# A state-space layer, routed experts, attention and a Kronecker MLP on one core: the last expert slot joins the tokens by one-hot products, and softplus is summed in PSUM by VectorE

## The chip, the core and the metric

The kernel runs on one NeuronCore of a Trainium2 chip. Its engines work side by side, each from its own in-order queue: TensorE (PE in the profile, with its weight loads as PEld), VectorE (DVE), ScalarE (ACT), GpSimd (POOL) and SyncE (SP, which issues most DMAs; ACT and POOL issue some too). The metric is device time in microseconds. Everything is float32. A measurement of this kernel can tell about 0.3% from no change.

## The reference, cut to what matters

Input x is (4, 384, 32, 32): four batches of 384 channels and 1024 positions. Two layers follow, each a token mixer and a channel mixer, with normalisation ahead and a residual around each.

```python
# layer 0, mixer: four directions k of a selective scan over 1024 positions, 16 states
dt = softplus(dts + dt_projs_bias)             # (4, 4, 384, 1024)
h  = h * exp(dt * A) + (dt * u) * B            # per position, (b, k, 384, 16)
y  = einsum('bkdn,bkn->bkd', h, C)
x  = x + gelu(layernorm(merge(y + D * u)))
# layer 0, experts: four experts 384 -> 1536 -> 384, two for each token
probs  = softmax(t @ gate_w + gate_b);  masked = top-2 of probs, normalised
t = t + sum_e masked[e] * (gelu(t_n @ w1[e] + b1[e]) @ w2[e] + b2[e])
# layer 1: attention of 8 heads with one projection for q, k and v, then an MLP
t = t + mlp(ln(x + attention(ln(x))))
```

## The kernel before

**Two strands.** `scan_layer` runs the scan of batch 0, then of 1, 2 and 3. `tail_batch` does the rest for one batch: routing (`route`, `spread`, `places`), experts (`experts`), the sum of each token's two expert rows (`combine`), attention, and the last layers. The tail of batch b-1 stands in the program behind the scan of batch b and runs beside scans; the tail of batch 3 runs at the end, in a second set of buffers (`wide`). The order of instructions on each engine isn't the order of the code: the program is built with `schedule_with_timeline_sim=True`, and a planner orders it by a simulated timeline, by the order of the code where several are ready, and `high_priority(offset=FORWARD)` moves a block ahead. Tiles that share a tag share a number of buffers (`NARROW`, `WIDE`), which are handed out as they come free; `got`, the weights `w1` and `w2`, and others share "kw" (8 buffers, 10 in `wide`), and `xs`, `xc`, `y`, `diag`, `ex` and others share "k4" (5, and 4 in `wide`).

**A scan.** It is cut into units of one direction and one half of the positions, eight for a batch, and each unit into three pieces of 128 channels (`chunk`), 24 pieces a batch. While one unit runs, `project` prepares the next. For a piece: a product gives the step sizes before softplus in a PSUM bank (`dt_ps`, L365); softplus is computed as max(z, 0) + ln(1 + e) + (e - ((1 + e) - 1)) with e = exp(-|z|), where the last bracket restores what rounding 1 + e lost; the result and its product with u go to HBM and come back spread over states (`dtr`). ScalarE makes |z| (L369), max(z, 0) (L370), e (L371), 1 + e (L372), its logarithm (L373). In batch 0 the terms are added in PSUM by identity products (L378). In the other batches ScalarE forms (1 + e) - 1 (L382), GpSimd makes two subtractions (L395, L396), and VectorE one addition in PSUM (L402). `behind` places the GpSimd and VectorE parts behind an instruction of the running piece. Then `chunk` does, for four groups of states: products on GpSimd (L440, L468), exponentials on ScalarE (L449), scans and products on VectorE (L454, L461), and sums over states on TensorE (L475).

**Routing.** `clear` writes zeros to a list of 2432 rows in HBM (`rows`, 19 writes of 128 rows). `places` finds for each token and each of its two experts a row, so that each block of 256 or 128 rows belongs to one expert. `spread` normalises the tokens and scatters each to its two rows (L685, 16 indirect DMAs on GpSimd).

**Experts.** There are 11 slots: 8 of 256 rows and 3 of 128. For each, `fetch` loads the weights of its expert and `gather` loads its rows and transposes them; then the first product (L954), Gelu, the second (L975), an addition of the bias (L979), and the rows are written to HBM (`made`, L982). The last slot's write is issued by ScalarE, the others by SyncE.

**Combine.** Two diagonal matrices of the gates are made on GpSimd (L996), 16 indirect DMAs on GpSimd fetch each token's two rows from `made` (L1005); they depend on all writes to `made`. `add` puts them onto the residual: two products with the diagonals (L1012) and an addition (L1015) for each 128 tokens, followed by the statistics for the next normalisation (L1037, L1038) in `prologue`.

**Attention.** Its row sums of exponentials are kept for all batches in `sums`; `overflow` takes one maximum of them at the end.

## Time and profile before

| what | value |
|---|---|
| median of 3 runs | 4249.24 us (4240.75 to 4253.25) |
| profiled execution | 4230.72 us |
| its span | 4228.9 us |
| scans 0, 1, 2, 3 (first to last product on GpSimd) | 30 to 685, 683 to 1557, 1557 to 2508, 2508 to 3408 us |
| experts of batches 0 to 3 (first to last product) | 862 to 1298, 1825 to 2257, 2793 to 3218, 3503 to 3930 us |
| first projection of attention, batches 0 to 3 | 1353, 2313, 3284, 3965 us |

A busy time is that of instructions in flight on an engine; matmul ends are modelled, and a product of float32 is recorded as two passes. In a group of instructions, "out<-in" names what is written and read, followed by the count, the busy time, the mean of one, and the idle time of the engine just before with what ended it. In an answer by windows each row has the stretch, its length, then busy time (and count) of PE, PEld, DVE, ACT and POOL, the granted clock, the DMA share and GB/s.

### The profile page before, as it was taken

The page shows a single profiled execution, that of the slowest core. Times are in us where ns is not written, and L with a number is a line of the kernel's source. Part 1 is how long each engine was busy: PE and PEld are TensorE (multiplying, and loading weights), DVE is VectorE, ACT ScalarE, POOL GpSimd, SP SyncE. Part 2 cuts the span into 40 slices and gives each one's busy share as a digit, 9 for nine tenths or more (in the row PEclk, how much of TensorE's full clock was granted, in tenths as well). Part 3 has the DMA queues.
Part 4 walks back from the last instruction along what each step waited for, and adds up shares of the span by engine and source line. Part 5 has one row for each costly group of instructions (what it writes and reads, how often), then busy time and mean ns, then how long its engine had stood idle before and what let it go on. Part 6 is the DMA issues. An engine that isn't in the chain of part 4 may idle for free.

```text
span 4228.9 us, 45721 instructions
## 1 busy us (share of the span) xinstructions
PE 3363.3 (80%) x13308; PEld 1581.4 (37%) x13308; DVE 2846.4 (67%) x4152; ACT 2505.9 (59%) x4494; POOL 3020.1 (71%) x1471
## 2 busy tenths in 40 slices
PE   6544545489897888789996888789996899999898
PEld 2111111155553223245553223245553235566323
DVE  5999997878887878788887777888886840010101
ACT  5555555556665776666665777676664763443353
POOL 5999997898988978789899878889897840000100
PEclk8666666589998999789997999789997899999999
DMA  5454464677886535667887434658887434255200
GB/s 138 125 135 123 117 174 109 187 218 218 242 249 176 153 106 147 198 178 230 251 247 220 130 100 133 200 166 242 227 250 225 117 107 143 86 174 209 64 16 31
DMA packets 410387, 693.70 MB, mean 164 GB/s; under 512 B 51088, under 2 KB 209680, under 8 KB 410128
## 3 DMA queue, kind: packets, MB, share of 16 engines
q1 hardware_dynamic: 399728, 662.71, 54.1%
q0 software_dynamic: 8192, 25.17, 1.8%
q10 hardware_dynamic: 2208, 2.82, 0.2%
q8 instruction: 107, 1.75, 0.2%
q14 instruction: 152, 1.25, 0.1%
HBM read 569.00 MB, written 121.50 MB: 163 GB/s over the span
## 4 chain that ended last, share of the span: by engine, by line
PE 37%; DVE 22%; ACT 11%; DMA 11%; POOL 9%; issue 7%; SPq 3%; DVEq 0%; POOLq 0%; ACTq 0%
PE y_ps L975 9%; PE h_ps L954 9%; DVE da L454 8%; DVE bx L454 7%; POOL bx L440 5%; DMA dtr<-dd 4%; ACT da L449 3%; PE s_ps L1099 3%; PE acc L475 3%; DVE bx L461 3%; PE o_acc L1145 3%; POOL bx L468 2%; DMA w<-in_w 2%; SPq L424 2%; DMA bcs<-both 1%
## 5 line engine op out<-in xcount | busy, mean ns | idle before, releaser
L440 POOL TENSOR_TENSOR bx<-dtr,bcs 128x1024 f32<-128x1024 f32 x768 | 1794.0, 2363 | 201.6 <-PE acc L475 92.4
L449 ACT ACTIVATE da<-dtr,nega 128x512 f32<-128x512 f32 x1536 | 1045.3, 690 | 898.3 <-DVE bx L461 540.9
L468 POOL TENSOR_TENSOR bx<-bx,bcs 128x1024 f32<-128x1024 f32 x384 | 905.1, 2362 | 133.3 <-DVE carry L465 60.5
L475 PE MATMUL acc<-bx,sel 128*32 128x512 f32 x3072 | 500.2, 697 | 294.0 <-POOL bx L468 256.8
L954 PE MATMUL h_ps<-xc,w 128*128 128x256 f32 (+1 forms) x3168 | 675.8, 370 | 71.0 <-DMA w<-in_w 40.0
L975 PE MATMUL y_ps<-w,hs 128*128 128x384 f32 x1824 | 634.4, 500 | 26.7 <-ACT hs L967 20.1
L954 PEld LDWEIGHTS h_ps<-xc,w 128*128 128x128 f32 x3168 | 561.0, 201 | 240.7 <-issue 120.2
L454 DVE TENSOR_TENSOR_SCAN bx<-da,carry,bx 128x512 f32<-128x512 f32 x384 | 473.5, 1270 | 112.9 <-ACT da L449 57.7
L454 DVE TENSOR_TENSOR_SCAN da<-da,carry,bx 128x512 f32<-128x512 f32 x384 | 477.3, 1275 | 60.9 <-ACT da L449 50.2
L454 DVE TENSOR_TENSOR_SCAN bx<-da,bx 128x512 f32<-128x512 f32 x384 | 453.5, 1211 | 90.4 <-ACT da L449 56.8
L461 DVE TENSOR_TENSOR bx<-da,bcs 128x512 f32<-128x512 f32 x768 | 511.0, 681 | 4.0
L454 DVE TENSOR_TENSOR_SCAN da<-da,bx 128x512 f32<-128x512 f32 x384 | 456.1, 1219 | 76.6 <-ACT da L449 64.8
L975 PEld LDWEIGHTS y_ps<-w,hs 128*128 128x128 f32 x1824 | 348.4, 195 | 306.2 <-issue 64.7
L1105 ACT ACTIVATE ex<-s_ps 128x512 f32<-128x512 f32 x512 | 300.8, 592 | 130.1 <-PE s_ps L1099 126.6
L1099 PE MATMUL s_ps<-w 64*128 64x512 f32 x1024 | 310.6, 664 | 61.6 <-ACT ex L1105 56.3
L962 ACT ACTIVATE hs<-h_ps,bb 128x256 f32<-128x256 f32 (+1 forms) x528 | 200.5, 441 | 212.4 <-PE h_ps L954 208.2
L996 POOL TENSOR_TENSOR diag<-ident,g_weight 128x1024 f32<-128x1024 f32 x8 | 15.0, 1896 | 424.3 <-PE xc_ps L936 410.6
L1145 PE MATMUL o_acc<-ex,vt 128*64 128x512 f32 x1024 | 284.7, 633 | 24.0 <-ACT ex L1105 16.8
L475 PEld LDWEIGHTS acc<-bx,sel 128*32 128x32 f32 x3072 | 75.8, 116 | 594.1 <-POOL bx L468 361.7
L979 DVE TENSOR_TENSOR y<-y_ps,bb 128x384 f32<-128x384 f32 x76 | 41.6, 547 | 230.9 <-PE y_ps L975 230.6
L1099 PEld LDWEIGHTS s_ps<-w 64*128 64x128 f32 x1024 | 83.8, 190 | 267.2 <-ACT ex L1105 219.0
L365 PE MATMUL dt_ps<-xd,wdt 108*128 108x512 f32 x192 | 123.1, 728 | 63.4 <-ACT mag L404 34.4
(222 smaller groups left out, 3613.0 us busy)
## 6 DMA issues: line engine op xcount, KB each, us to landing
w<-in_w SPq DMA_DIRECT2D x352, 576.0 KB
dtr<-dd SPq DMA_DIRECT2D x1536, 128.0 KB
bcs<-both SPq DMA_DIRECT2D x512, 128.0 KB
dd<-one_e SPq DMA_DIRECT2D x96, 256.0 KB
dd<-mag SPq DMA_DIRECT2D x96, 256.0 KB
rows<-zero SPq DMA_DIRECT2D x76, 192.0 KB
xt<-x SPq DMA_DIRECT2D x32, 384.0 KB
made<-y SPq DMA_DIRECT2D x32, 384.0 KB
```

Source lines behind the costliest of these rows:

```text
L440: pool = nc.gpsimd.tensor_mul(bx, dtr[q][1], bc[:, 0].unsqueeze(1).to_broadcast([P, 2, HF])).ins
L449: nc.scalar.activation(da, dtr[q][0][:, j, :], AF.Exp, scale=nega[:, col : col + 1])
L454: nc.vector.tensor_tensor_scan(run(h), run(da), run(bx[:, j, :]), 0.0 if first else hold, ALU.mult, ALU.add,)
L461: dve = nc.vector.tensor_mul(bx[:, j, :], h, cg).ins
L468: pool = nc.gpsimd.tensor_mul(bx, bx, cg.unsqueeze(1).to_broadcast([P, 2, HF])).ins
L475: nc.tensor.matmul(acc[lo : lo + DB, :], sel, out[q][:, j, :], start=(g == 0), stop=(g == NG - 1),)
L954: ins = nc.tensor.matmul(ps[:, r, :], w1[(f + r) // wf][:, c, (f + r) % wf * P : ((f + r) % wf + 1) * P], xc[:, c, :], start=(c == 0), sto ...
L962: done = nc.scalar.activation(hs[:, f + r, :], ps[:, r, :], AF.Gelu if last else AF.Identity, bias=bb[:, f + r : f + r + 1],).ins
L975: nc.tensor.matmul(out[:, :D], hs[:, f, t * P : (t + 1) * P], w2[f // wf][:, f % wf, :], start=(f == 0), stop=(f == FC - 1),)
L1099: ins = nc.tensor.matmul(ps, w[rows, j * P : (j + 1) * P], w[rows, halves(i)], start=True, stop=True).ins
L1105: done.append(nc.scalar.activation(ex[:, o, :], ps, AF.Exp, scale=HD**-0.5, accum_out=sums[:, t, 2 * j + o, i : i + 1],).ins)
L1145: ins = nc.tensor.matmul(out[cols, :], made[t][1][:, j, cols], ex[:, o, :], start=(j == 0), stop=(j == MB - 1),).ins
```

## The change

- The bias of softplus enters through the product: row 44 of the product's weights (`XD`, zero before) holds the bias, and row 44 of the other operand holds ones, which the copy of `xd` adds as a column of the identity matrix. The bias operands go.
- In batches 1 to 3, ScalarE no longer forms max(z, 0) and (1 + e) - 1, GpSimd makes no subtractions, and VectorE makes three two-operation passes in PSUM in the place of one addition.
- The last slot's rows are not written to `made`. Each row of the list gets a 385th column with the number of its token plus one (zero where there is none), so rows are 1540 bytes long. When the last slot's rows are loaded, VectorE compares this number with the numbers of each 128 tokens: eight one-hot matrices (`own`). In `combine`, eight products of these with the slot's result, and eight multiply-adds with the gate of the token's row in this slot (`near`), add them to the residual. The 16 gathers take row 0 with weight zero where a token's row lies in the last slot.
- The maximum of the row sums is taken for each batch (`tops`).

```diff
+STORED = NROW - P
+W = D + 1
+WC = max(w for w in range(1, P + 1) if W % w == 0)
...
-            nc.scalar.copy(xd, ps[:XP, :])
+            nc.scalar.activation(
+                xd, ps[:XP, :], AF.Identity, bias=self.ident[:XP, XD : XD + 1]
+            )
...
-            bias = self.col("dtb", k * DC + c)
             mag, one_e, lnw = k2("mag"), k2("one_e"), k2("lnw")
-            relu = k2("relu") if b == 0 else ps
-            nc.scalar.activation(mag, ps, AF.Abs, bias=bias)
-            nc.scalar.activation(relu, ps, AF.Relu, bias=bias)
+            nc.scalar.activation(mag, ps, AF.Abs)
+            if b == 0:
+                relu = k2("relu")
+                nc.scalar.activation(relu, ps, AF.Relu)
...
-            else:
-                nc.scalar.activation(one_e, one_e, AF.Identity, bias=self.minus1)
...
-            if b > 0:
-                with behind("pool"):
-                    nc.gpsimd.tensor_sub(mag, one_e, mag)
-                    nc.gpsimd.tensor_sub(lnw, lnw, mag)
             yield
...
                 if b > 0:
-                    nc.vector.tensor_add(ps, ps, lnw)
+                    stt(ps, ps, 0.0, lnw, ALU.max, ALU.add)
+                    stt(ps, one_e, 1.0, ps, ALU.subtract, ALU.subtract)
+                    stt(ps, ps, -1.0, mag, ALU.mult, ALU.add)
...
-                out=self.rows[b][at : at + P, :].rearrange("p (c d) -> p c d", c=DC),
-                in_=self.zero.unsqueeze(1).to_broadcast([P, DC, P]),
+                out=self.rows[b][at : at + P, :].rearrange("p (c d) -> p c d", d=WC),
+                in_=self.zero[:, :WC].unsqueeze(1).to_broadcast([P, W // WC, WC]),
...
+                xt = room.tile([P, 2, W], "k4", "xt")
+                nc.sync.dma_start(out=xt[:, :, :D], in_=self.tokens(b)[:, m : m + 2, :])
+                nc.scalar.copy(xt[:, :, D:], self.number[:, m : m + 2].unsqueeze(2))
...
+        nc.vector.tensor_scalar(stored, place, float(STORED) - 0.5, None, op0=ALU.is_lt)
+        nc.vector.tensor_mul(place, place, stored)
...
+        nc.vector.tensor_copy(source, place)
...
+        nc.vector.tensor_mul(weight, both, stored)
...
+        nc.vector.tensor_sub(rest, both, weight)
...
+        nc.vector.tensor_reduce(near, rest.rearrange("p k m -> p m k"), AX.X, ALU.add)
+        return pos, expert, (source, weight, near)
...
+            if s == NSLOT - 1:
+                apart = room.tile([P, MB], "apart", "apart")
+                nc.vector.tensor_sub(apart, xs[:, 0, D:].to_broadcast([P, MB]), self.full)
+                own = room.tile([P, MB, P], "k4", "own")
+                for m in range(MB):
+                    nc.vector.tensor_scalar(
+                        own[:, m, :], self.column, apart[:, m : m + 1], None, op0=ALU.is_equal
+                    )
+                self.own = own
...
-            queue = nc.sync if s + 1 < NSLOT else nc.scalar
-            queue.dma_start(
-                out=made[at : at + size, :].rearrange("(t p) d -> p t d", p=P), in_=y
-            )
+            if s + 1 < NSLOT:
+                nc.sync.dma_start(
+                    out=made[at : at + size, :].rearrange("(t p) d -> p t d", p=P), in_=y
+                )
+        return self.own, y
...
+        own, y = last
+        for m in range(MB):
+            ps = room.bank("p", "n_ps")[:, :D]
+            nc.tensor.matmul(ps, own[:, m, :], y[:, 0, :], start=True, stop=True)
+            nc.vector.scalar_tensor_tensor(
+                xt[:, m, :], ps, near[:, m : m + 1], xt[:, m, :], op0=ALU.mult, op1=ALU.add
+            )
```

## The prediction

> **What bounds the kernel now.** I read the page's busy times first, then cut the span into stages at the first and last instruction of each step of the tail (expert products, combine, attention, last layers) and asked for the busy times of those stretches, then the groups of instructions that the change touches, then the instructions in order of time at the end of the last batch's experts.
>
> From the page:
>
> ```profile
> PE 3363.3 (80%) x13308; PEld 1581.4 (37%) x13308; DVE 2846.4 (67%) x4152; ACT 2505.9 (59%) x4494; POOL 3020.1 (71%) x1471
> ```
>
> No engine is full over the whole span, so the stages decide. The busy time by stretch (us; then PE, weight loads, DVE, ACT, POOL, granted clock, DMA share, GB/s):
>
> ```profile
> 30.00:685.00 655.00, 341.66 (x1013) 91.72 (x1011) 576.38 (x789) 349.53 (x544) 609.38 (x265) 0.68 0.51 134
> ...
> 1299.00:1353.00 54.00, 31.08 (x88) 12.91 (x85) 36.85 (x54) 23.24 (x43) 49.27 (x33) 0.72 0.62 175
> 1353.00:1634.00 281.00, 239.69 (x993) 67.36 (x991) 225.15 (x292) 216.09 (x480) 242.02 (x114) 0.95 0.45 125
> ...
> 1825.00:2257.00 432.00, 397.23 (x1743) 250.41 (x1742) 354.98 (x478) 287.97 (x459) 386.00 (x180) 0.95 0.83 239
> 2257.00:2313.00 56.00, 27.87 (x99) 12.57 (x97) 38.96 (x60) 24.97 (x45) 49.38 (x33) 0.66 0.62 170
> ...
> 3218.00:3284.00 66.00, 35.59 (x99) 13.20 (x94) 42.04 (x79) 27.34 (x49) 52.98 (x35) 0.70 0.63 179
> ...
> 3930.00:3965.00 35.00, 20.00 (x56) 10.35 (x57) 10.61 (x27) 7.99 (x18) 15.32 (x16) 0.80 0.45 140
> ```
>
> The first scan has no tail beside it and is POOL's (93% busy, PE at half). From 862 us on the tails of the four batches follow each other without a gap while scans 1 to 3 run beside them until 3435. In expert stages PE is 92% busy at a clock of 0.95, so PE ends them; POOL is 89% and DVE 82% busy there. The 54, 56, 66 and 35 us stretches are the combines, from the last expert product to the first projection of attention: PE is idle for 23, 28, 30 and 15 us of them, and the clock falls. That is what the change can shorten.
>
> The groups of softplus, and POOL's largest (busy, mean ns | idle before):
>
> ```profile
> L440 POOL TENSOR_TENSOR bx<-dtr,bcs 128x1024 f32<-128x1024 f32 x768 | 1794.0, 2363 | 201.6 <-PE acc L475 92.4 <-DMA dtr<-dd 80.1 <-issue 20.2
> ...
> L395 POOL TENSOR_TENSOR mag<-one_e,mag 128x512 f32<-128x512 f32 x72 | 92.0, 1278 | 35.1 <-ACT one_e L382 35.1
> L396 POOL TENSOR_TENSOR lnw<-lnw,mag 128x512 f32<-128x512 f32 x72 | 91.9, 1276 | 0.3
> ...
> L382 ACT ACTIVATE one_e<-one_e,minus 128x512 f32<-128x512 f32 x72 | 51.5, 715 | 0.5
> L402 DVE TENSOR_TENSOR dt_ps<-dt_ps,lnw 128x512 f32<-128x512 f32 x72 | 49.5, 688 | 15.2 <-POOL lnw L396 15.2
> ...
> L370 ACT ACTIVATE dt_ps<-dt_ps,cols 128x512 f32<-128x512 f32 x72 | 47.1, 654 | 0.0
> ```
>
> And the last combine in order of time (start, us):
>
> ```profile
> 3929.66 0.56 DVE L979 TENSOR_TENSOR y<-y_ps,bb 128x384 f32<-128x384 f32 x1 [13.73 <-PE y_ps L975]
> 3930.25 0.34 ACTq L982 DMA_DIRECT2D made<-y  x1
> 3932.91 1.01 POOL L1005 DMA_INDIRECT got<-made,g_pos  x1 [12.44 <-DMA made<-y]
> ...
> 3953.60 0.95 POOL L1005 DMA_INDIRECT got<-made,g_pos  x1 [0.30 <-issue]
> ```
>
> The write of the last slot lands 2.66 us after its issue; only then do 16 gathers start, one every 1.26 us, and attention begins 11.7 us after the last of them was issued.
>
> **The change, part by part.** The sum is made against the profiled execution, 4230.7 us, 18.5 us under the median of the three runs; I add it back at the end.
>
> *Combine, last batch.* The gathers now wait for the slot before: its write was issued at 3915.96 and POOL, which waited for it, went on at 3918.57, 14.3 us sooner than now. Sixteen at 1.26 us end at about 3939 instead of 3954.5. Their buffers are those of the weights ("kw", ten in this room): the last two or three must wait for the last slot's second product, half done at 3925.6, so this start holds. New work stands after the last product (3929.6): its addition, then eight one-hot products. Sixteen passes of the old combine took 5.72 us, so a pair of passes takes 0.72 us and eight 5.7 us; eight additions by VectorE at 0.55 us (row L1015) run behind them, the last at about 3936.7. Then the old per-token work, 0.55 + 0.56 + 0.18 = 1.3 us on VectorE for each of eight tiles, ends at 3947.3 against 3960.9 now. It isn't all gained, since the transposes of the first half stand in PE's queue between: I take 10 of the 13.6 us. Bounds: nothing gained, or all 14.
>
> *Combine, batches 0 to 2.* Here the room has eight "kw" buffers, all held by the last slot's weights, so eight gathers can start after its first product and eight only as its second ends. Now the first gather starts 15.4, 10.2 and 31.2 us after the last product: in batch 0 ScalarE issued the write only at 1303.32, 5 us after the addition began, because its queue stood behind a wait for DVE (10.1 us); in batch 2 five multiplications of the scan (11.6 us) are ordered ahead of the gathers on POOL. Without the write, and with half of the 20 us of gathers gone ahead, some 15 to 30 us go; the one-hot products and their additions give back 6.5, longer where DVE is busy with scans. I take 12, 12 and 20 us. What is late next is DVE: nothing starts before its eight additions. Bounds per batch: 5 lost (products added, gathers ordered as late as now), 25 gained.
>
> *Softplus of batches 1 to 3, 72 pieces.* Gone: two ScalarE passes (47.1 + 51.5 = 98.6 us), two of POOL (92.0 + 91.9 = 183.9 us and 35.1 us of its waiting), one of DVE (49.5). New: three DVE passes over PSUM. The nearest row is L402 itself, an addition in PSUM at 688 ns; other two-operation forms on 512 columns took 681 to 738. 72 x 3 x 0.688 = 148.6 us, net +99.1 us on DVE (bounds 97 to 110), or 33 us for each scan. Per piece of a scan (24 a batch) POOL now does 12 x 2.36 + 2.55 = 30.9 us and DVE 16 x 1.24 + 8 x 0.68 + 1.2 of carries + 2.2 = 28.7; afterwards POOL does 28.4 and DVE 30.1. With the tail's own share (about 1.8 and 1.9 us a piece) the larger one goes from 32.7 to 32.0, so neither gets shorter by much: the bound passes from POOL to DVE. Pieces last 36.4 us (874 us of scan 1 over 24), and PE hides both where it is 92% busy. In the attention stages ScalarE, whose queue waits 541 us in all for DVE's multiplications, loses 1.4 us a piece while DVE's clump before it grows by 1.4. I put nothing on the whole of it. Cover gone, it would cost up to 99 us; POOL's relief, if POOL is what paces, is worth up to 61 - 33 = 28 us a batch, 84 us.
>
> *The bias in the product, batch 0.* The Abs and Relu rows lose a bias operand (679 and 680 ns with it); the sixteen copies of xd (580 ns) become biased passes (about 680): +1.6 us on ScalarE, hidden in a scan that is POOL's. Nothing, or 2 us.
>
> *Routing.* Four small ScalarE copies a batch (0.17 us, row L541) stand ahead of the scatters, 1 us a batch on the path: 4 us. Seven small DVE operations (about 0.2 us each) come after the positions and eight comparisons with a sum (under 0.3 us each, 128 columns) beside the last slot: 4 us of DVE a batch, covered by PE's products. Scatters and slot loads move 1540 instead of 1536 B a row: nothing. The sum's maximum per batch: one small DVE operation, nothing.
>
> *The clears.* A row of zeros goes in five pieces of 308 B, not three of 512: 76 x 640 = 48,640 pieces for 29,184. The trace's 512 B packets took 27.8 ns on average, 4 B packets 9 ns, so the sixteen engines' time goes from 50.7 us to between 27 and 85 us, at most 8.5 us more a batch; issue on SP (0.64 us each) may grow too. Three clears stand in the first scan and in attention stages (DMA share 0.5), but the last (3205 to 3225) stands in SP's queue just ahead of the last scan's loads: I take 2 us, bounds -2 to 9. The Trainium skill (DMA: Bandwidth & Descriptors, Specifications) speaks against this edit: it wants 512 B or more, since smaller transfers are read, modified and written. By an estimate from it, with each piece twice the time of a 512 B one, a clear would need 42 us instead of 13 and cost the last batch some 20; no row here shows such a piece, and the sum goes without it.
>
> Sum: -10 - 44 + 4 + 2 = -48 us. 4230.7 - 48 = 4183 in the profiled execution, and 4249.2 - 48 = **4201 us** as a median.
>
> **Rivals.**
> *DVE becomes the bound and the kernel slower.* Place: scans 1 to 3, where DVE is already 82% busy and ScalarE waits for it 541 us. Three passes in one clump delay the next scan, then ScalarE's exponentials and attention behind them. Three quarters of the 99 us showing gives 4201 + 74 = 4275. The gain is used up when about half (48 of 99) shows. Against it: ScalarE gets 99 us shorter and PE ends the expert stages.
> *POOL paced the scans.* For it: 89% busy, 99% in the first scan, and 35 us of waits on it vanish. If 60 of the 84 us show: 4140. Against it: tails, not scans, run to the end, and PE is busy there.
> *The gathers do not come sooner.* They still stand behind scan work in POOL's queue or behind the buffers of the weights. Then 2.7 us of write are saved four times (11) and 4.5 us of additions are added four times (18), with routing 6: 4262. Against it: in the last batch POOL is idle for 12 us before the first.
>
> **How the numbers follow.** The likeliest: 0.45, with its own range 4170 to 4240 (combine 20 to 75, the rest 0 to 10). DVE 0.23, POOL 0.18, gathers 0.14. A measurement here can tell about 0.3% (the three runs spread by 12.5 us). Faster: 0.42 of the likeliest and POOL's 0.18, 0.60. Same: 0.03 of the likeliest, 0.07 of the gathers' case, 0.03 of DVE's, 0.13. Slower: 0.20 and 0.07, 0.27. The range, 4130 to 4290, takes in POOL's case and most of DVE's.
>
> **What would show it.** Combine stretches of about 25, 42, 44 and 46 us (last batch first), with the last batch's first gather before the last expert addition; POOL near 2836 us busy, DVE near 2965 (99 and some 20 for additions and comparisons), ScalarE near 2410; expert stages unchanged at 425 to 437 us. I am wrong if these grow with DVE above 90%, if scans 1 to 3 get shorter by over 30 us each, or if the order of instructions, which is planned anew for the changed program, puts a wait into a queue that holds the scans up.

## The result and the profile after

The changed kernel takes 4393.89 us (median; 4388.52 to 4401.94) against 4242.99 us (4240.75 to 4253.25) for the kernel before: a ratio of 1.0352, with an interval of 1.0335 to 1.0369. It is 151 us slower, where 48 us faster was forecast. The profiled execution has a span of 4392.1 us. From its page:

```profile
PE 3407.5 (78%) x13372; PEld 1588.5 (36%) x13372; DVE 2951.4 (67%) x4394; ACT 2420.3 (55%) x4364; POOL 2844.5 (65%) x1328
...
DMA packets 429266, 693.01 MB, mean 158 GB/s; under 512 B 99664, under 2 KB 228560, under 8 KB 429008
```

The work is what the prediction said: DVE 2951 us (2965 forecast), ScalarE 2420 (2410), POOL 2844 (2836). PE is busy 44 us longer than before (64 more passes, and somewhat longer ones); at most that much of the 151 us can be added work. The bytes are those of before, but packets under 512 B went from 51088 to 99664.

The prediction shows the expert stage of batch 1 before; those of batches 0 and 2 before are:

```profile
862.00:1298.00 436.00, 400.41 (x1741) 250.10 (x1741) 354.65 (x485) 284.36 (x455) 383.38 (x177) 0.95 0.81 233
2793.00:3218.00 425.00, 391.22 (x1729) 247.82 (x1727) 344.10 (x469) 283.90 (x452) 375.36 (x173) 0.95 0.82 237
```

The stretches of after, in the columns of the prediction's windows (a stretch in the first scan; expert stages of batches 0, 1 and 2; last combine):

```profile
30.00:740.00 710.00, 347.48 (x1053) 94.88 (x1051) 602.52 (x823) 359.47 (x567) 633.17 (x276) 0.70 0.53 129
921.00:1395.00 474.00, 415.98 (x1782) 253.86 (x1781) 406.91 (x545) 291.92 (x464) 391.99 (x174) 0.93 0.78 225
1995.00:2485.00 490.00, 418.99 (x1783) 256.29 (x1782) 392.49 (x540) 290.38 (x462) 367.53 (x162) 0.92 0.85 227
3045.00:3491.00 446.00, 402.56 (x1738) 253.56 (x1738) 314.27 (x483) 250.27 (x401) 295.88 (x136) 0.95 0.84 227
...
4079.00:4133.00 54.00, 46.35 (x154) 19.38 (x151) 20.56 (x43) 33.38 (x45) 2.62 (x2) 0.84 0.15 56
```

In the first of these stretches POOL is busy for 633 of 710 us, in the first scan's stretch of before for 609 of 655. The two do not hold the same work (276 and 265 POOL instructions), so their lengths can't be compared. A scan's own length is read from POOL's 192 products at L440, first to last. By these, scans 0 to 3 ran from 45 to 749, 752 to 1629, 1629 to 2528 and 2530 to 3408 us before; the ends that the table of before gives for the first three (685, 1557 and 2508) are too early. In after they ran from 44 to 773, 780 to 1642, 1650 to 2552 and 2555 to 3397. So the first scan got 25 us longer, the second 15 us shorter, the third 3 us longer and the last 35 us shorter. Expert stages grew from 434, 429 and 421 us to 474, 490 and 446, and PE is 85 to 90% busy in them, down from 92. The combines are 78, 64, 39 and 54 us long; the last of them holds work of batch 2's last layers, which had not fallen so late before.

The waits that grew most are those of ScalarE's exponentials and of POOL's products in the scans. The second product and the exponentials before (the first product stands in the prediction), then all three in after:

```profile
L449 ACT ACTIVATE da<-dtr,nega 128x512 f32<-128x512 f32 x1536 | 1045.3, 690 | 898.3 <-DVE bx L461 540.9 <-DVE bx L454 251.3 <-DMA dtr<-dd 61.6
L468 POOL TENSOR_TENSOR bx<-bx,bcs 128x1024 f32<-128x1024 f32 x384 | 905.1, 2362 | 133.3 <-DVE carry L465 60.5 <-DVE bx L454 57.4 <-DVE carry L460 9.4
```

```profile
L440 POOL TENSOR_TENSOR bx<-dtr,bcs 128x1024 f32<-128x1024 f32 x768 | 1792.0, 2360 | 289.6 <-DMA dtr<-dd 164.8 <-PE acc L475 103.1 <-issue 14.6
L449 ACT ACTIVATE da<-dtr,nega 128x512 f32<-128x512 f32 x1536 | 1044.2, 689 | 1118.7 <-DVE bx L461 723.1 <-DVE bx L454 297.4 <-DVE carry L465 40.8
L468 POOL TENSOR_TENSOR bx<-bx,bcs 128x1024 f32<-128x1024 f32 x384 | 903.9, 2358 | 273.5 <-DVE carry L465 126.1 <-DVE bx L454 111.2 <-DVE carry L460 12.6
```

ScalarE waits 723 us for VectorE's multiplications (541 before). POOL's second product waits 273.5 us, nearly all of it for VectorE (133.3 before), and its first waits 165 us for the step sizes that come back from HBM (80 before). A last view tells which strand ends the kernel. From the end of scan 3's products to the last experts, attention and last layers, first before, then after:

```profile
3408.00:4224.00 816.00, 767.46 (x3095) 389.28 (x3087) 93.04 (x221) 354.13 (x764) 43.08 (x40) 0.97 0.32 107
```

```profile
3397.00:4386.00 989.00, 952.89 (x3865) 481.34 (x3863) 121.63 (x302) 432.86 (x955) 61.90 (x58) 0.98 0.34 113
```

Scan 3 ends at nearly the same time in both (3408 and 3397 us). What is left then is 989 us instead of 816, with PE 96% busy: the tails had fallen behind by 185 us of PE work, and no scan is left beside which to do it.

### The profile page after: what moved, and what is told of

Read it like the earlier page. It is cut to its first block, busy times and chain, and to the rows that moved or that the text cites. A ratio compares the mean times of both kernels' runs of the same rounds, so it can differ in the third digit from the quotient of the medians.

```text
span 4392.1 us, 45640 instructions
## 1 busy us (share of the span) xinstructions
PE 3407.5 (78%) x13372; PEld 1588.5 (36%) x13372; DVE 2951.4 (67%) x4394; ACT 2420.3 (55%) x4364; POOL 2844.5 (65%) x1328
## 5 line engine op out<-in xcount | busy, mean ns | idle before, releaser
L440 POOL TENSOR_TENSOR bx<-dtr,bcs 128x1024 f32<-128x1024 f32 x768 | 1792.0, 2360 | 289.6 <-DMA dtr<-dd 164.8
L468 POOL TENSOR_TENSOR bx<-bx,bcs 128x1024 f32<-128x1024 f32 x384 | 903.9, 2358 | 273.5 <-DVE carry L465 126.1
L475 PE MATMUL acc<-bx,sel 128*32 128x512 f32 x3072 | 524.0, 702 | 395.2 <-POOL bx L468 331.9
L980 PE MATMUL h_ps<-xc,w 128*128 128x256 f32 (+1 forms) x3168 | 685.7, 371 | 75.8 <-DMA w<-in_w 23.5
L1001 PE MATMUL y_ps<-w,hs 128*128 128x384 f32 x1824 | 643.3, 504 | 42.2 <-ACT hs L993 24.5
L1032 POOL DMA_INDIRECT got<-made,g_source x64 | 61.2, 956 | 600.6 <-PE x_var L1261 525.6
```

The source lines that it names most:

```text
L440: pool = nc.gpsimd.tensor_mul(bx, dtr[q][1], bc[:, 0].unsqueeze(1).to_broadcast([P, 2, HF])).ins
L468: pool = nc.gpsimd.tensor_mul(bx, bx, cg.unsqueeze(1).to_broadcast([P, 2, HF])).ins
L475: nc.tensor.matmul(acc[lo : lo + DB, :], sel, out[q][:, j, :], start=(g == 0), stop=(g == NG - 1),)
L980: ins = nc.tensor.matmul(ps[:, r, :], w1[(f + r) // wf][:, c, (f + r) % wf * P : ((f + r) % wf + 1) * P], xc[:, c, :], start=(c == 0), sto ...
L1001: nc.tensor.matmul(out[:, :D], hs[:, f, t * P : (t + 1) * P], w2[f // wf][:, f % wf, :], start=(f == 0), stop=(f == FC - 1),)
```

## The experiments

Ratios are to the kernel before, measured beside each kernel on the same chip; brackets are 95% intervals. The kernel before took between 4242.8 and 4245.8 us (medians) there, but 4271.85 us beside four kernels: softplus with the tail after the sixth unit, the last slot with the tail after the third, the last slot with held gathers, and the whole change with the tail after the fourth. What made these runs of the kernel before 0.65% longer isn't known: the granted clock is the usual one (0.871 against 0.873), the profiles of the four show no slower transfers, and the same chip later gave 4243.92 us. So it isn't known either whether the four kernels were slowed with it, and for them both the ratio and the time are given.

### Which part costs it

**after with 512 B clears.** The same number of zeros, in 385 pieces of 512 B from 77 partitions:

```diff
-                out=self.rows[b][at : at + P, :].rearrange("p (c d) -> p c d", d=WC),
-                in_=self.zero[:, :WC].unsqueeze(1).to_broadcast([P, W // WC, WC]),
+                out=self.rows[b][at : at + P, :].rearrange("p d -> (p d)").rearrange(
+                    "(q c d) -> q c d", q=W // DCL, d=P
+                ),  # DCL = 5
+                in_=self.zero[: W // DCL, :].unsqueeze(1).to_broadcast([W // DCL, DCL, P]),
```

> The changed kernel, but a write of zeros goes in 385 pieces of 512 B (from 77 partitions) in the place of 640 of 308 B. In the changed kernel the 308 B pieces took 57 ns each (512 B ones took 27.8 before), SyncE needed 25 to 40 us for a batch's 19 issues, and the DMA share reached 0.98 beside them. Theory C (the clears): most of the 151 us is theirs, so 4235 to 4290 us, pieces back at about 28 ns, the first scan ending near 690 us. Theory V (the three passes on VectorE hold up scans and attention): the clears give back only their own 40 to 60 us, 4330 to 4360. Theory O (the order planned anew): no prediction of size, but stages far from any clear stay as slow as in the changed kernel.

**The softplus part alone**, on the kernel before (bias through the product, no ScalarE passes for max(z, 0) and (1 + e) - 1, no POOL subtractions, three passes on VectorE):

```diff
-                    nc.vector.tensor_add(ps, ps, lnw)
+                    stt(ps, ps, 0.0, lnw, ALU.max, ALU.add)
+                    stt(ps, one_e, 1.0, ps, ALU.subtract, ALU.subtract)
+                    stt(ps, ps, -1.0, mag, ALU.mult, ALU.add)
```

> The kernel before with the softplus part alone (bias in the product, three passes of VectorE in PSUM for batches 1 to 3); experts, rows and clears as before. Theory C: no clear is touched, so 4190 to 4255 us. Theory V: 4300 us or more, with expert and attention stages of batches 0 to 2 each 15 us or more longer.

**The last slot alone, with the 512 B clears** (the first kernel with its softplus put back):

```diff
-                    stt(ps, ps, 0.0, lnw, ALU.max, ALU.add)
-                    stt(ps, one_e, 1.0, ps, ALU.subtract, ALU.subtract)
-                    stt(ps, ps, -1.0, mag, ALU.mult, ALU.add)
+                    nc.vector.tensor_add(ps, ps, lnw)
```

> The kernel before with the last slot's part alone (385 columns, one-hot products, last slot not written), with clears in pieces of 512 B; softplus as before. Theory C and theory V both: 4190 to 4255 us, the combines shorter by the 10 to 20 us each that I forecast. If it is slower than 4260, the last slot's part costs by itself, and what it costs is read from the combine and expert stages.

**The kernel before with clears in 384 B pieces**, four to a row in the place of three of 512 B:

```diff
-                out=self.rows[b][at : at + P, :].rearrange("p (c d) -> p c d", c=DC),
-                in_=self.zero.unsqueeze(1).to_broadcast([P, DC, P]),
+                out=self.rows[b][at : at + P, :].rearrange("p (c d) -> p c d", d=96),
+                in_=self.zero[:, :96].unsqueeze(1).to_broadcast([P, D // 96, 96]),
```

> The kernel before, with the zeros of a row written in four pieces of 384 B in the place of three of 512 B; nothing else. Theory C: a piece takes about twice the 27.8 ns, so a batch's clear takes some 35 us of all sixteen engines in the place of 13, and the kernel 4280 to 4360 us. Theory V: 4240 to 4255, since nothing of VectorE's work changes.

| kernel | median, us | ratio to before |
|---|---|---|
| after, 512 B clears | 4355.97 | 1.0262 [1.0228, 1.0296] |
| softplus alone | 4305.96 | 1.0146 [1.0110, 1.0182] |
| last slot alone, 512 B clears | 4319.77 | 1.0179 [1.0148, 1.0211] |
| before, 384 B clears | 4276.40 | 1.0072 [1.0050, 1.0095] |

Each part costs by itself: neither the softplus part nor the last slot gains anything alone. The last slot's loss agrees with neither theory. 384 B pieces were cheap for the DMA engines (22.3 ns each, 54.1 us of sixteen engines' time against 50.7 before) and for SP (0.66 us a write, 0.64 before), so theory C's price was not there; and yet that kernel lost 31 us, which theory V had not foreseen either. Its trace runs the order of before, with a first scan of 705 us (704 before), up to about 1443 us, in the attention of batch 0; after that the order is another. That raised the suspicion that any edit upsets the order and costs a per cent.

### Is it the new order alone?

Two edits that do next to nothing, meant to change the plan: a VectorE memset of one column at the start of batch 1's scan, and a GpSimd one at the starts of scans 1 to 3.

```diff
-            us = {0: start(0)}
+            us = {0: start(0)}; spare = wp.tile([P, 1], F32, tag="spare", name="spare")
...
-                b, k, i = unit
+                b, k, i = unit; None if n != KG * NH else nc.vector.memset(spare, 0.0)
```

> The kernel before with one VectorE memset of one column (some 0.1 us) at the start of batch 1's scan. It does no work to speak of, but the planner orders the program anew: the written order of VectorE differs in 192 rows of 3433, that of ScalarE in 193. Theory O (a new order alone costs some per cent of what was lost, because the order before was a good one): 4265 to 4320 us. Theories C and V, which need work or bytes: 4235 to 4255.

```diff
-                b, k, i = unit
+                b, k, i = unit; None if n % (KG * NH) != KG else nc.gpsimd.memset(spare, 0.0)
```

> The same with one GpSimd memset of one column at the start of the scans of batches 1 to 3. Theory O: 4265 to 4320 us, and not the same as with the VectorE one. Theories C and V: 4235 to 4255.

4245.89 us, 0.9992 [0.9973, 1.0012], and 4242.31 us, 0.9987 [0.9970, 1.0004], as fast as before. But they do not answer the question. The written order differed in some 190 places, as the first of the two texts says; in the traces of both kernels PE, VectorE, ScalarE and POOL run the operations of before in exactly the order of before, apart from the added memsets. So they ran no new order, and what one costs was not tested by them. Two other kernels bear on it. The columns without the one-hot part (below) run another order from about 800 us on and lose nothing (0.9988), so a new order can be free. The 384 B clears lost 31 us, 0.72%, with the pieces themselves and the new order after 1443 us as the only differences from before that their trace shows; that a new order can cost that much is the likeliest reading, but it isn't shown. It stays a rival of that size for the losses below.

### The clears

First the columns without the one-hot part: 385 columns, the number of the token, 512 B clears and the routing's extra operations, but the last slot written and gathered as before.

```diff
-STORED = NROW - P
+STORED = NROW
...
-                own = room.tile([P, MB, P], "k4", "own")
...
-            nc.tensor.matmul(ps, own[:, m, :], y[:, 0, :], start=True, stop=True)
```

> The kernel before with rows of 385 columns, the token's number, the clears in 512 B pieces and the routing's extra operations, but with the last slot written and gathered as before: no one-hot matrices, no products with them. If the 74 us of the last slot's part come from the longer rows and the routing: 4300 to 4325. If they come from the one-hot matrices, their products and the order of the combine: 4245 to 4270.

4237.03 us, 0.9988 [0.9973, 1.0003]: columns, number and routing are free. Then the same kernel, with the clears of after, and with each row cleared in one piece of 1540 B:

```diff
-                out=self.rows[b][at : at + P, :].rearrange("p d -> (p d)").rearrange(
-                    "(q c d) -> q c d", q=W // DCL, d=P
-                ),
-                in_=self.zero[: W // DCL, :].unsqueeze(1).to_broadcast([W // DCL, DCL, P]),
+                out=self.rows[b][at : at + P, :].rearrange("p (c d) -> p c d", d=WC),
+                in_=self.zero[:, :WC].unsqueeze(1).to_broadcast([P, W // WC, WC]),
```

> Rows of 385 columns, last slot written and gathered as before, and clears in five pieces of 308 B as in the changed kernel. With 512 B pieces this kernel took 0.9988 of the time of the one before. Theory C: 1.005 to 1.015 of it (the changed kernel lost 38 us by these pieces), a piece again at 50 to 60 ns on average and SyncE held for 25 us or more by a batch's clear. If the pieces cost only beside the one-hot part: 0.998 to 1.003.

```diff
-        self.zero = wp.tile([P, P], F32, tag="zero", name="zero")
+        self.zero = wp.tile([P, W], F32, tag="zero", name="zero")
...
-                out=self.rows[b][at : at + P, :].rearrange("p d -> (p d)").rearrange(
-                    "(q c d) -> q c d", q=W // DCL, d=P
-                ),
-                in_=self.zero[: W // DCL, :].unsqueeze(1).to_broadcast([W // DCL, DCL, P]),
+                out=self.rows[b][at : at + P, :], in_=self.zero,
```

> The same with each row cleared in one piece of 1540 B, from a tile of zeros 385 wide. If odd addresses as such make writes slow, a piece takes well over the 75 ns that pieces of 1536 B take, and the kernel 1.003 or more of the one before. If it is small pieces that share an odd boundary, a piece takes 65 to 90 ns and the kernel 0.995 to 1.001.

4359.67 us, 1.0262 [1.0245, 1.0279], with 308 B pieces, more than the text above allowed; 4239.80 us, 0.9987 [0.9974, 1.0001], with 1540 B. The shape of the clears alone costs 2.7% of this kernel, some 116 us. The trace says how. A 308 B piece took 57 ns on average in after (median 27) and 69 ns here (median 42); the four clears held the sixteen engines for 174 and 210 us. On SP's queue, the first batch's 19 writes before and after (start, duration):

```profile
534.07 12.89 SPq L599 DMA_DIRECT2D rows<-zero  x19
```

```profile
534.39 33.46 SPq L602 DMA_DIRECT2D rows<-zero  x19
```

One write took 0.64 us to issue before; in after the median of the 19 shown is 1.9 us, and that of all 76 is 1.7 us. The scan's loads of step sizes stand behind them in the same queue. POOL in after, just after that clear, and both kernels in the 60 us around it (before, then after):

```profile
584.94 6.95 POOL L440 TENSOR_TENSOR bx<-dtr,bcs 128x1024 f32<-128x1024 f32 x3 [24.31 <-DMA dtr<-dd]
```

```profile
530.00:590.00 60.00, 24.05 (x81) 5.29 (x78) 55.26 (x76) 30.19 (x47) 59.58 (x27) 0.59 0.76 198
```

```profile
530.00:590.00 60.00, 10.24 (x40) 1.30 (x36) 32.73 (x37) 13.42 (x20) 34.69 (x16) 0.61 1.18 155
```

POOL loses 25 of these 60 us, and the DMA share rises to 1.18 while fewer bytes move (155 against 198 GB/s). In the columns kernel it is the same: POOL's first product with 512 B pieces, then with 308 B ones (the same line, here L446):

```profile
L446 POOL TENSOR_TENSOR bx<-dtr,bcs 128x1024 f32<-128x1024 f32 x768 | 1794.7, 2364 | 210.1 <-PE acc L481 88.4 <-DMA dtr<-dd 84.3 <-issue 17.7
```

```profile
L446 POOL TENSOR_TENSOR bx<-dtr,bcs 128x1024 f32<-128x1024 f32 x768 | 1793.2, 2361 | 315.7 <-DMA dtr<-dd 152.6 <-PE acc L481 127.6 <-issue 17.5
```

It waits 106 us more, 68 of them for step sizes. With the columns alone, scans 0 to 3 took 708, 892, 909 and 874 us; with 308 B pieces 734, 906, 945 and 905, and scan 3 ends 107 us later: most of the price lies in the scans. The first 26 us are the clear's alone, since the two kernels run the same order until about 1456 us; after that the order differs too. How the price divides between engines and queue was not measured.

The pieces need to be seen by the row. A row of three 512 B pieces took 81 ns of an engine before (27 each), a row in one piece of 1540 B took 97 ns on average (median 73), and a row of five 308 B pieces 286 ns in after and 345 here. So the single piece was slower than the text above allowed for a harmless one, and the kernel lost nothing all the same. Small pieces of 384 B in rows of 1536 B were cheap, whole rows of 1540 B nearly so, and 308 B pieces in rows of 1540 B dear. Why, the records don't show.

### Softplus: scans faster, kernel slower

In the softplus part alone, scan 3 ends at 3307 us, 101 us sooner than before: POOL's relief did speed the scans. Its stretches (experts of batches 0, 1, 2; then the rest after scan 3):

```profile
893.00:1355.00 462.00, 408.93 (x1783) 250.04 (x1783) 399.81 (x538) 291.76 (x464) 386.27 (x167) 0.94 0.77 229
1917.00:2390.00 473.00, 420.47 (x1783) 256.79 (x1784) 396.84 (x552) 297.26 (x468) 381.42 (x166) 0.94 0.78 234
2953.00:3394.00 441.00, 399.74 (x1767) 255.53 (x1767) 333.83 (x508) 264.41 (x419) 311.75 (x140) 0.95 0.75 231
3307.00:4297.00 990.00, 925.65 (x3797) 466.71 (x3795) 108.02 (x259) 430.88 (x947) 61.85 (x57) 0.97 0.34 112
```

The expert stages grew by 28, 44 and 20 us, and after scan 3 there are 990 us left, not 816. The time is in the range of theory V. Is it the passes or the relief? One kernel takes the relief but makes one VectorE pass instead of three, the other keeps GpSimd's part and adds two neutral passes:

```diff
                     stt(ps, ps, 0.0, lnw, ALU.max, ALU.add)
-                    stt(ps, one_e, 1.0, ps, ALU.subtract, ALU.subtract)
-                    stt(ps, ps, -1.0, mag, ALU.mult, ALU.add)
```

> The softplus part alone, without the two VectorE passes that restore the rounding of 1 + e (left out of the computation here): GpSimd and ScalarE are relieved as in the softplus part, VectorE does one pass in the place of one. Theory V: the loss of 60 us is the two passes', so 4190 to 4250 us. Rival S (scans that run faster take PE, ScalarE and VectorE from the tails, which are what ends last): 4280 us or more, with scans shorter than in the softplus part and expert stages above 450 us.

```diff
                     nc.vector.tensor_add(ps, ps, lnw)
+                    for _ in range(2):
+                        nc.vector.scalar_tensor_tensor(
+                            ps, lnw, 0.0, ps, op0=ALU.mult, op1=ALU.add
+                        )
```

> The kernel before with two more VectorE passes in PSUM that change nothing, for each piece of batches 1 to 3 (99 us of VectorE in all), GpSimd and ScalarE as before. Theory V: 4290 us or more (50 us and up). Rival S: the scans get slower, not faster, so the tails lose nothing: 4240 to 4270.

4259.41 us, 1.0032 [1.0016, 1.0048], and 4257.19 us, 1.0025 [1.0005, 1.0046]. Two passes more cost 11 us; the relief without them brings no gain but a loss of 14 us, though scan 3 then ends 153 us sooner than before. That lies between the ranges of theory V and rival S, while the two passes alone came out as rival S said. Together they cost 62, and why 14 and 11 make 62 isn't shown. The expert stages don't tell it: with one pass they are 471, 463 and 441 us long, as long as the 462, 473 and 441 with three, and about 1000 us are left after scan 3 in both. The 48 us between these two kernels lie in the scans, which end at 3254 and 3307 us. What can be said is that a faster scan is no gain here, because the tails end the kernel. If the tails lose by running beside faster scans, giving the tails their place earlier should undo it. The experts of batch b-1 stand in the program behind scan b; these two kernels, softplus alone and the kernel before, have them after the third of its eight units:

```diff
+                if b > 0 and n % (KG * NH) == 2:
+                    between(-b)
...
-                if b > 0:
-                    body.tail_batch(b - 1, x1, room)
+                if b < 0:
+                    if b == -1:
+                        body.moe_consts(room)
+                        for step in body.route(0, x1, room):
+                            step()
+                    body.xc = body.first_layer(-b - 1, room)
+                elif b > 0:
+                    body.second_layer(b - 1, body.xc, room, body.route(b, x1, room))
```

> The softplus part alone, with the experts of batch b-1 written into the program after the third unit of scan b (eight units) in the place of its end, so that the planner puts them ahead of the rest of that scan. Theory S (the tails end last, and scans that got faster took their time from them): expert stages of batches 0 to 2 go from 462, 473 and 441 back to 435 or less, scans get longer, and the kernel 4306 to 4200 to 4260. Theory V (VectorE's passes are too much work): no better than 4290.

> The kernel before with its experts written into the program at that same earlier place, softplus as before. Theory S: the tails gain here too, 4180 to 4235 us. If scans and tails were already balanced in the kernel before: 4235 to 4300.

4253.89 us, 1.0030 [1.0018, 1.0041], and 4260.93 us, 1.0042 [1.0027, 1.0057]. With experts first, their stages take 400, 401 and 393 us with softplus and 402, 386 and 398 without, and the two kernels are equal. The scans pay for it, as expected: with softplus scans 1 to 3 take 889, 936 and 915 us, and POOL's first product waits 248 us for PE's sums (92 before). So the loss of 1.46% belongs to softplus only with the tail at the end of the scan's code. The kernel before gained nothing from the earlier place, where theory S let it gain 8 us or more; so there the two strands were already in balance, as the second text's other reading has it. A place in between, after the sixth unit:

```diff
-                if b > 0 and n % (KG * NH) == 2:
+                if b > 0 and n % (KG * NH) == 5:
```

> The softplus part alone, with the experts written after the sixth unit of the scan (after the third they gave 4254, at the end 4306). Theory S: scans and tails are in balance somewhere between, so 4200 to 4260 us, with expert stages between 400 and 460. If the place acts only by a chance of order, no trend: anything from 4240 to 4310.

4308.67 us, 1.0095 [1.0066, 1.0123]. By the ratio it lies between the other two, by the time it gains nothing (4305.96 us at the end), so the place in between settles nothing. The place after the third unit, against the end, does: the place of the tail's code, which is its rank where several instructions are ready, decides the loss. Whether it does so by the rank itself, or because that program came out in a better order, these runs don't tell apart, and by what step a faster scan holds up a late tail wasn't traced.

### The last slot: the combine did not get shorter

The last slot alone has combines of 57, 58, 57 and 36 us, against 55, 56, 66 and 36 before. Its last one, in order of time:

```profile
4006.39 0.98 POOL L1040 DMA_INDIRECT got<-made,g_source  x1 [444.82 <-issue]
...
4019.04 0.56 DVE L1013 TENSOR_TENSOR y<-y_ps,bb 128x384 f32<-128x384 f32 x1 [15.70 <-PE y_ps L1009]
...
4019.65 5.43 PE L1047 MATMUL n_ps<-y,own 128*128 128x384 f32 x16 [0.65 <-DVE y L1013]
...
4027.99 3.75 POOL L1031 TENSOR_TENSOR diag<-ident,g_weight 128x1024 f32<-128x1024 f32 x2
4029.95 0.50 PEld L1055 LDWEIGHTS w_ps<-got,diag 128*128 128x128 f32 x2 [5.49 <-POOL diag L1031]
```

The first gather does start 12.7 us ahead of the last addition, where it had started 3.3 us behind it, and the one-hot products run at once. But the diagonal matrices of the gates, which before were made ahead of the gathers, now stand behind all sixteen of them on POOL, and the first half's products wait for them until 4029.95, 10.9 us after the addition. The second half's products come later still, once the first half's transposes are done:

```profile
4044.12 5.55 PE L1055 MATMUL w_ps<-got,diag 128*128 128x384 f32 x16 [0.25 <-ACT xc L1098]
```

They start 25.1 us after the last expert product; before it was 24.2. In batch 0 the gathers came early too (the last was issued at 1326.6 us), and there the second half's additions ran on VectorE only at 1348.5 to 1356.8, between the scan's own operations. One-hot matrices and diagonals share the "k4" buffers, so the last batch's one-hot tile was given a buffer of its own:

```diff
-                own = room.tile([P, MB, P], "k4", "own")
+                own = room.tile([P, MB, P], "own" if room.name == "w" else "k4", "own")
```

> The last slot's part alone with 512 B clears, and for the last batch (whose room has the space) the one-hot matrices in a buffer of their own, not one of k4's four. Theory K (the one-hot matrices hold the buffer that the gates' diagonals need, so GpSimd makes these after the 16 gathers): the last combine falls from 36 to 22 to 28 us and the kernel by 8 to 14 us against the 4320 of the last slot's part alone, the diagonals standing ahead of the gathers. If the combine stays at 36, the chain of sums on VectorE and the transposes set it, not the diagonals.

4310.85 us, 1.0162 [1.0136, 1.0187], not distinguishable from 1.0179; its last combine is 38 us, and the diagonals still come last:

```profile
4021.86 0.94 POOL L1040 DMA_INDIRECT got<-made,g_source  x1 [0.30 <-issue]
4022.83 3.75 POOL L1031 TENSOR_TENSOR diag<-ident,g_weight 128x1024 f32<-128x1024 f32 x2
```

So it is not that buffer alone. The last slot's result `y`, which now lives on in a "k4" buffer until the combine, is another candidate and was not tried; why the planner leaves the diagonals behind the gathers wasn't found. The combines explain a gain that did not come, not a loss of 76 us. That lies beside the scans: scan 3 ends 66 us later than before, and scan 2 alone takes 945 us instead of 899. Two experiments: experts after the third unit, and gathers held back until the last slot's addition, as they were before.

```diff
+                if b > 0 and n % (KG * NH) == 2:
+                    between(-b)
```

> The last slot's part alone with 512 B clears, and the experts written after the third unit of the scan. With them at the end it took 4320. If its loss is that of scans going ahead of tails: 4240 to 4270. If it lies in the one-hot work, its buffers and the combine: 4295 or more.

```diff
-                nc.vector.tensor_add(y[:, t, :], out[:, :D], bb[:, FC:])
+                self.summed = nc.vector.tensor_add(y[:, t, :], out[:, :D], bb[:, FC:]).ins
...
-                nc.gpsimd.indirect_dma_start(
+                took = nc.gpsimd.indirect_dma_start(
...
+                ).ins
+                self.depend(took, self.summed)
```

> The last slot's part alone with 512 B clears, and each gather made to wait for the bias addition of the last slot, so that none stands early in GpSimd's queue. If the early gathers hold the scans up: 4255 to 4290 us. If the one-hot work and its buffers cost the 74 us: 4320 to 4370, since the gathers' head start is gone as well.

4304.79 us, 1.0073 [1.0045, 1.0101], and 4311.01 us, 1.0091 [1.0064, 1.0118]; the last slot alone took 4319.77 us. By the ratios, holding the gathers back recovers half of the loss; by the times 9 of its 76 us, and 4311.01 us lies in neither range of its text. The trace doesn't show that the early gathers took the scans' time: with held gathers scan 3 ends at 3498 us, later than the 3474 with early ones, and what got shorter is the rest after it (814 us against 842) and batch 0's attention (281 us against 323). With the tail early, 0.73% remain by the ratio, of which 0.42% is that place's own price, or 61 us by the time. So neither edit settles what the last slot's part does beside the scans: its cause stays open.

Last, the whole change with 512 B clears and experts after the fourth unit:

```diff
+                if b > 0 and n % (KG * NH) == 3:
+                    between(-b)
```

> The whole change with 512 B clears, and the experts written after the fourth unit of the scan. With them at the end it took 4356. Theory S: softplus's 60 us go, the last slot's stay in part, 4270 to 4310 us. If both losses are matters of which strand goes first: 4230 to 4265. If the work itself costs it: 4330 or more.

4337.40 us, 1.0153 [1.0119, 1.0187] (4355.97 us, 1.0262 with the given order). Clears and place together take it from 3.5 to 1.5% by the ratio; by the time 93 of the 151 us are left. The rest stays open. No version here beats the kernel before; the columns with 512 B or 1540 B clears equal it.

## Why the prediction was wrong

- *The clears.* "I take 2 us, bounds -2 to 9" was the worst term: 116 us alone, and 38 us inside the whole change (1.0352 against 1.0262), where the parts hide some of each other (116, 62 and 76 add up to 254, and the whole is 151). The bound came from 512 B and 4 B packets, taken as if a price followed size (9 ns for 4 B is the median; the mean is 11.6); the pieces cost twice the larger. Nor was only the last clear exposed, as the prediction said: each of the four held up the loads behind it, the first too, in a scan with POOL full. In the columns kernel scans 0 to 3 got 26, 14, 36 and 31 us longer. The prediction's own estimate of 42 us a clear, worked out from the Trainium skill (DMA: Bandwidth & Descriptors, Specifications) with twice the time for each piece, met the measured 174 / 4 = 43.5 us of the sixteen engines. That may be luck: that transfers below 512 B cost more isn't what 384 B pieces showed (22.3 ns against 27.8), and half of the 308 B pieces took 27 ns or less.
- *Softplus.* The sizes were right: three passes at 681 to 685 ns (688 taken), DVE +105 us with the rest. "I put nothing on the whole of it", with PE's expert stages as the cover, was wrong: 62 us. The prediction saw a choice between DVE pacing the scans and POOL pacing them. Two more passes alone cost 11 us, not the 74 of the first rival. POOL did pace them, and scans got 101 us faster; but the prediction's own remark against that rival, "tails, not scans, run to the end", holds more than it was used for. In the given order the kernel got 62 us slower, though its scans were faster, and with the tail's code after the third unit it lost nothing (1.0030 against 1.0042). PE at 92% in expert stages was read as a cover; it was a strand with its own 8% of waits, which could grow. The step from one pass (14 us) to three (62 us) isn't explained by the stages of experts, and a part of it may be a new order's own price.
- *Combine.* "-10 - 44" came to 9 us in batch 2 alone: by the part alone 57, 58, 57 and 36 us, that is 2 and 2 us more, 9 less and none. The last batch's gathers did start early, so the step that failed is what they were to release: products that then waited for the diagonals, for the first half's transposes, and in batch 0 for VectorE. The first gather, which had come 15.4, 10.3, 31.2 and 3.3 us after the last expert product of its batch, now came 10.1 and 1.3 us ahead of it, 2.3 behind and 12.6 ahead. (Attention began 11.5 us after the last gather's issue before, not 11.7; nothing rests on it.) So the rival "the gathers do not come sooner" fell in all four batches, and the part alone still lost 76 us, where that rival lost 13. The sum had no term for what the slot's part does beside the scans; scan 3 ended 66 us later with it, and why stays open.
- *Routing, columns, sums, bias.* "4 us" and nothing: right within the measurement for routing and columns (0.9988). The comparisons took a median of 278 ns (under 300 said) but a mean of 513; the additions after the one-hot products 609 ns (550 taken). Both small.
- *The planned order.* Named at the end as what could make it wrong. The new order of the columns kernel cost nothing (0.9988); the 384 B clears lost 31 us, and beside the pieces, which were cheap, the new order is the only difference from before that their trace shows. The place of the tail in the code decided what the softplus part cost.

## What to carry to other kernels

Where two strands share in-order engines, ask first which of them ends last: making the other faster can cost more than it brings, until the order of the program is changed with it. When a transfer's pieces change, their price can't be taken from pieces of another size and pitch; time such pieces, and look at what stands behind them in their queue. A row that becomes one element longer turned a cheap write of this kernel into the dearest edit. Where the stages of the trace of before show what bounds them, ask too what the cover is worth when it grows by a tenth: here the expert stages did, and the softplus term, put at nothing behind them, came to 62 us. And when an edit is made to test an order, look in its trace whether the order that ran is another.

## What the runs showed of the hardware

- Writes of zeros in 308 B pieces at a row pitch of 1540 B: 57 and 69 ns a piece on average (median 27 and 42), against 27.8 ns for 512 B (all packets of that size before; 27.0 for the clears alone), 22.3 ns for 384 B in rows of 1536 B, and 97 ns (median 73) for whole rows of 1540 B. By the row that is 286 and 345, 81, 89 and 97 ns.
- SP took a median of 1.7 us in after, and 1.9 us in the columns kernel, to issue one such write of 640 pieces; 0.64 us for 384 pieces of 512 B, 0.66 us for 512 pieces of 384 B, 0.88 us for 385 of 512 B from 77 partitions and 0.44 us for 128 pieces of 1540 B. The number of pieces alone doesn't explain it.
